# Layer 1 of a two-layer graph network on one core: the lower halves of x are taken against a copy in PSUM

## The chip, the core and the metric

The kernel runs on one core of a Trainium2 chip. The metric is device time in microseconds (us) for one execution. Before the change the median of 14 runs is 1414.99 us (1411.05 to 1419.32). TensorE (PE) multiplies and writes to PSUM, which has 8 banks of 512 f32 values in each of 128 partitions; VectorE (DVE) and ScalarE (ACT) read and write SBUF and PSUM; GpSimd (POOL) issues the gathers; SyncE (SP), ACT and POOL each issue DMAs in their own order. Each engine works through one list in order and meets the others at semaphores.

## What is computed

x has 6250 rows of 256 numbers. An edge list of 100,000 pairs (src, dst), sorted by dst, adds row src to row dst. The low dst numbers have by far the most edges.

```python
def _gin_agg(h, src, dst, eps, n_nodes):
    agg = jax.ops.segment_sum(h[src], dst, num_segments=n_nodes)
    return (1.0 + eps) * h + agg
...
h = _gin_agg(x, src, dst, eps1, n)         # layer 1, width 256
h = jax.nn.relu(h @ W1a + b1a)             # 256 -> 512
h = jax.nn.relu(h @ W1b + b1b)             # 512 -> 512
h = _gin_agg(h, src, dst, eps2, n)         # layer 2, width 512
h = jax.nn.relu(h @ W2a + b2a)
out = h @ W2b + b2b                        # 512 -> 256
...
x = _layernorm(x + out, axis=-1)
```

## The kernel before

Nodes are cut into 49 tiles of 128 (the last has 106), edges into 782 chunks of 128. After a preparation (index transposes, checks on the data) the program runs `layer` twice, for layer 1 and layer 2. The instruction order of every engine is fixed when the program is built, by a planner in Python: a clock that advances one `tick` per gathered chunk, work that is put off by some ticks (`later`), and two queues (`blockwise`, `beside`) that get credit with each chunk and spend it on work priced in estimated microseconds.

Three streams run beside each other in a layer.

- Gathers, for the edges of the lighter tiles: L270 issues one indirect DMA on POOL's queue per chunk, which brings the 128 rows named by `srcs` into one of `PIECES * BURST` = 24 places in the tile `early` (layer 1). The PE adds them up with a selection matrix (L1109). A gather into a place that is still used waits for the matmul that reads it, 24 chunks earlier. The sums leave PSUM through ACT (`split`, L1133), go through a second matmul (L1158) and are added to `acc` on DVE (L1147).
- Products, for the seven heaviest tiles (`HEAVY`): how often each source node occurs is counted in `counting` (DVE comparisons L939 and L942, matmul L985, DVE addition L955 into `at`). ACT turns the counts of one heavy tile and one range of four node tiles into the matrix `cf` (L970), and the PE multiplies it with the rows of x of that range (L885). To keep precision, x is handed to the PE in two halves of type f32r: an upper one (x rounded) and a lower one (x minus the upper), which stand side by side in the tile `both`. The heavy tiles are done in four passes, [6,5], [4], [3,2], [1,0], each over 13 ranges, so the halves are made 4 x 13 = 52 times, in `cut`. `both` has two buffers; `cut` is called for the current turn and the one after it before the current turn's matmuls are issued.
- Blocks of two finished tiles: transpose (L745), ACT copy to `zt` (L754), matmul with W1a (L777), ACT relu to `ht` (L786), matmul with W1b (L798), DVE bias (L1184), ACT relu (L1188), store of `h1`.

PSUM is handed out by the bank. `place` takes the first bank from the list `empty`; when the list is empty it first runs, at once, the put-off work that is due soonest among that which frees a bank. `take_later` puts off the reading of a bank by `LAG` = 10 ticks (7 for the sums of gathers), and `free` puts the bank at the end of the list.

```python
def place(n):
    while not empty:
        undelay(min((d for d in delayed if d[2]), key=lambda d: d[0]))
    i = empty.pop(0)
    return banks[i][:, :n], i
```

`halve` (L535, L536) makes the two halves: an ACT copy into the upper half, then a DVE subtraction. Layer 1 calls it from `cut` once per range for all four tiles (128 x 1024); layer 2 calls it from its own branch of `cut` and from `add_groups`, whose subtraction reads a PSUM bank (`split<-bank,split`).

Of the kernel before, what the change touches and what calls it, by code (L numbers as in the profile page):

```python
# [9 lines left out]
F32 = mybir.dt.float32  # L10
# [3 lines left out]
ALU = mybir.AluOpType  # L14
# [23 lines left out]
BANK = 512  # L38
# [108 lines left out]
def tile_gin_residual_layernorm(  # L147
# [38 lines left out]
    nc = tc.nc  # L186
# [104 lines left out]
    with tc.tile_pool(name="prep", bufs=2) as prep, tc.tile_pool(  # L291
# [76 lines left out]
        for i, c in enumerate(range(NC2, NCP, 512)):  # L368
            n = min(512, NCP - c)
# [6 lines left out]
        for g0, g1 in runs:  # L376
            c, h = groups[g0]
            n = g1 - g0
            a, b = c - NC2, c - NC2 + PARTS * h * n
            of_run = heads[:, a:b].rearrange("p (g b h) -> p g b h", b=PARTS, h=h)  # L380
            nc.vector.tensor_copy(base[:, g0:g1], of_run[:, :, 0, 0])
            for j in range(PARTS):
# [19 lines left out]
                op=ALU.subtract,  # L402
# [50 lines left out]
        for a, b, n in taken:  # L453
# [6 lines left out]
                op=ALU.subtract,  # L460
# [67 lines left out]
    def rows(t):  # L528
        return min(P, N - t * P)

    def halve(upper, lower, of):

        nc.scalar.copy(upper, of)  # L535
        nc.vector.tensor_tensor(lower, of, upper, op=ALU.subtract)  # L536
# [18 lines left out]
    def ordered(ctx):  # L555
# [9 lines left out]
        def layer(number, ctx, table, width, scale, wa, ba, wb, wide, prepare, finish, conclude, fetch):  # L565
# [110 lines left out]
            def undelay(item):  # L676
                delayed.remove(item)
                item[1]()
# [17 lines left out]
# [7 lines that stand above are left out]
            def free(p):  # L703
                empty.append(p[1])

            def take_later(p, what, lag=LAG):

                def take():
                    what(p[0])
                    free(p)  # L710

                later(lag, take, frees=True)
# [95 lines left out]
            def products(turns, table_of, ready=lambda t: True):  # L808

                loaded = {}  # L810
                factors = []
                sums = {}

                def load(i):
                    r, t = turns[i]
                    ks = ranges[r]
                    n = len(ks)
                    if (i == 0 or turns[i - 1][0] != r):
                        xr = dense.tile([P, RANGE, width], F32 if once else F32R, tag="xr", name="xr", bufs=2 if once else 2)
                        raw = xr if once else xr.bitcast(F32)  # L820
                        whole = min(n, N // P - ks[0])
                        if whole:
                            nc.sync.dma_start(
                                raw[:, :whole, :],
                                table[ks[0] * P : (ks[0] + whole) * P, :].rearrange(
                                    "(k p) d -> p k d", p=P
                                ),
                            )
                        if whole < n:
                            k = ks[-1]  # L830
                            nc.sync.dma_start(raw[: rows(k), whole, :], table[k * P : N, :])
                        loaded[0] = [xr, None, ks]
                    factors.append((loaded[0], None, table_of(r, ks, t)))

                def cut(of):


                    xr, upper, ks = of
                    if upper is not None:
                        return  # L840
                    if once:
                        of[1] = both = dense.tile([P, RANGE, 2, width], F32R, tag="both", name="both", bufs=2)
                        n = sum(rows(k) == P for k in ks)
                        for m, js in ((P, slice(0, n)), (rows(ks[-1]), slice(n, len(ks)))):
                            if js.start < js.stop:
                                halve(both[:m, js, 0, :], both[:m, js, 1, :], xr[:m, js, :])
                        return
                    of[1] = upper = dense.tile([P, RANGE, width], F32R, tag="upper", name="upper")
                    whole = xr.bitcast(F32)
                    for j, k in enumerate(ks):  # L850
                        m = rows(k)
                        halve(upper[:m, j, :], xr[:m, j, :], whole[:m, j, :])

                load(0)
                yield 0.0
                for i, (r, t) in enumerate(turns):
                    while len(factors) < 5 and i + len(factors) < len(turns):
                        new = turns[i + len(factors)][0] != turns[i + len(factors) - 1][0]
                        if once and new and sum(
                            f[0][1] is None and f[0] is not factors[k - 1][0]  # L860
                            for k, f in enumerate(factors)
                        ) >= 2:
                            break
                        load(i + len(factors))
                    while not ready(t):
                        yield 0.0
                    for f in range(min(2, len(factors))):
                        cut(factors[f][0])
                        if factors[f][2] and ready(turns[i + f][1]):
                            cf = dense.tile([P, RANGE, P], F32R, tag="cf", name="cf", bufs=3 if once else 4)  # L870
                            factors[f][2](cf)
                            factors[f] = factors[f][0], cf, None
                    (xr, upper, _), cf, _ = factors.pop(0)
                    ks = ranges[r]
                    opens = not once or r == 0
                    closes = not once or r == len(ranges) - 1
                    if opens:
                        sums[t] = place(2 * width if once else width)
                    pm = sums[t]
                    for j, k in enumerate(ks):  # L880
                        m = rows(k)
                        sides = (upper,) if once else (upper, xr)
                        for l, of in enumerate(sides):
                            of = of[:m, j]
                            nc.tensor.matmul(  # L885
                                pm[0], cf[:m, j, :],
                                of.rearrange("p a b -> p (a b)") if once else of,
                                start=(opens and j == 0 and l == 0),
                                stop=(closes and j == len(ks) - 1 and l == len(sides) - 1),
                            )  # L890

                    def add_product(ap, t=t):
                        for l in range(2 if once else 1):
                            nc.vector.tensor_tensor(
                                acc[t], ap[:, l * width : (l + 1) * width], acc[t], op=ALU.add
                            )
                        left[t] -= 1

                    if closes:
                        take_later(pm, add_product)  # L900
                    yield (4 if once else 2) * PASS * len(ks) * width
# [8 lines left out]
            def counting():  # L910
# [69 lines left out]
                def step():  # L980
# [12 lines left out]

                last = {t: END[ts[-1]] for ts in PASSES for t in ts}
                product = products(
                    [(r, t) for ts in PASSES for r in range(len(ranges)) for t in ts],
                    convert, lambda t: added > last[t],
# [75 lines left out]
            if number == 1:  # L1073
                work += 8.0 + STEP * NC + ADD * len(STEPS)
                aside = counting()
            else:
                aside = products([(r, t) for r in range(len(ranges)) for t in heavy],
                                     load_counts)
# [11 lines left out]
            both = (blockwise, beside)  # L1090
            upto = 0
            together_ = []
            for k, g in enumerate(order):
# [76 lines left out]
                if k + 2 < len(order):  # L1170
                    n = len(members[order[k + 1]])
# [339 lines left out]
```

## Time and profile before

One profiled execution took 1410.88 us, and its span (first to last instruction of the program) is 1409.2 us; the mean granted TensorE clock is 0.942 of full speed. All times of the trace are us from the start of the span.

| engine | busy us | share of the span | instructions |
|---|---|---|---|
| PE | 1204.7 | 85% | 5929 |
| DVE | 901.2 | 64% | 2267 |
| ACT | 486.8 | 35% | 892 |
| POOL | 1016.5 | 72% | 1034 |

| what | from | to |
|---|---|---|
| gathers of layer 1 (502) | 9.6 | 673.4 |
| upper halves on ACT, first and last start (L535) | 124.9 | 629.6 |
| subtractions on DVE, first and last start (L536) | 133.5 | 630.1 |
| gathers of layer 2 (518) | 705.2 | 1368.2 |

Between 673.4 and 705.2 POOL waits 31.8 us for the store of `h1`, whose rows layer 2 gathers. In the views a line of a group gives source line, engine, operation, out<-in by tile names, the count, then busy us and mean ns of one, then the idle time of the engine just before these instructions and what ended it. PE busy time is modelled and overlaps between matmuls, so a PE at 95% need not be at its peak. "Idle ... <-issue" means that nothing the profile shows was waited for.

### The profile page before, as it was taken

How to read it: one execution, taken by the hardware profiler on the slowest of the kernel's cores; microseconds unless marked ns; L12 is line 12 of the kernel's file. 1: busy time of each engine (PE TensorE's matmuls, PEld its weight loads, DVE VectorE, ACT ScalarE, POOL GpSimd, SP SyncE). 2: the span in 40 equal slices, each digit the busy share in tenths (PEclk: the TensorE clock that was granted, in tenths of full speed). 3: DMA queues.
4: the chain of work that ended last, by engine and by line, in shares of the span. 5: the costliest groups of instructions: out<-in, count | busy, mean ns of one | idle time of the engine just before them, and what ended most of it. 6: DMA issues, size and time to landing. Idle time of an engine off the chain costs nothing. (4 is left out here: it accounts for less than half of the span.)

```text
span 1409.2 us, 18558 instructions
## 1 busy us (share of the span) xinstructions
PE 1204.7 (85%) x5929; PEld 723.9 (51%) x5929; DVE 901.2 (64%) x2267; ACT 486.8 (35%) x892; POOL 1016.5 (72%) x1034
## 2 busy tenths in 40 slices
PE   2589999889898788788844999999989999997977
PEld 1144554444454443454521666676656666663646
DVE  7998778799968667332126577868856555553323
ACT  0223652444245332672314234333323333321112
POOL 6777777777777777777076777777777777777760
PEclk9989999899999999899977899999999999998989
DMA  4645766666457555674398699888889989877761
GB/s 102 199 135 182 240 205 178 188 205 203 146 182 223 169 153 153 218 224 131 114 352 286 204 302 302 267 295 286 254 286 303 302 273 341 256 229 239 223 203 40
DMA packets 159242, 309.77 MB, mean 220 GB/s; under 512 B 25378, under 2 KB 89762, under 8 KB 159136
## 3 DMA queue, kind: packets, MB, share of 16 engines
q0 software_dynamic: 65536, 201.65, 46.1%
q1 hardware_dynamic: 73060, 82.55, 18.3%
q10 hardware_dynamic: 20540, 24.28, 5.1%
q8 instruction: 50, 0.82, 0.2%
q14 instruction: 56, 0.46, 0.1%
HBM read 279.57 MB, written 28.83 MB: 219 GB/s over the span
## 5 line engine op out<-in xcount | busy, mean ns | idle before, releaser
L270 POOL DMA_INDIRECT early<-in_x_dram,srcs x502 | 511.1, 1018 | 159.0 <-issue 130.1
L270 POOL DMA_INDIRECT early<-h,srcs x262 | 254.8, 973 | 111.3 <-issue 62.7
L270 POOL DMA_INDIRECT late<-h,srcs x256 | 248.0, 969 | 80.7 <-issue 64.0
L1147 DVE SCALAR_TENSOR_TENSOR acc<-bank,mask,acc 128x512 f32<-128x512 f32 (+1 forms) x421 | 231.6, 606 | 89.6 <-PE bank L1158 89.3
L1109 PE MATMUL bank<-early,sel 128*32 128x256 f32 (+1 forms) x1528 | 161.4, 499 | 79.9 <-DMA early<-in_x_dram,srcs 31.5
L798 PE MATMUL bank<-w1b_s,ht 128*128 128x512 f32 (+1 forms) x392 | 181.1, 608 | 3.6 <-ACT ht L786 2.9
L777 PE MATMUL bank<-zt,w2a_s 128*128 128x256 f32 (+2 forms) x800 | 182.6, 385 | 1.1 <-ACT zt L754 1.1
L777 PEld LDWEIGHTS bank<-zt,w2a_s 128*128 128x128 f32 x800 | 152.7, 196 | 38.8 <-issue 10.0
L1158 PE MATMUL bank<-split,to 128*128 128x512 f32 (+3 forms) x362 | 122.4, 445 | 26.6 <-ACT split L535 23.0
L885 PE MATMUL bank<-upper,cf 128*128 128x512 f32 (+1 forms) x294 | 123.9, 421 | 12.5 <-ACT cf L906 11.7
L955 DVE TENSOR_TENSOR at<-bank,at 128x490 f32 x173 | 115.1, 666 | 11.9 <-ACT cf L970 4.2
L885 PE MATMUL bank<-both,cf 128*128 128x512 f32 (+1 forms) x343 | 111.1, 452 | 13.1 <-ACT ht L786 8.6
L798 PEld LDWEIGHTS bank<-w1b_s,ht 128*128 128x128 f32 (+1 forms) x392 | 74.3, 195 | 91.9 <-issue 76.2
L786 ACT ACTIVATE ht<-bank,b2a_s 128x256 f32<-128x256 f32 (+2 forms) x100 | 41.4, 465 | 221.1 <-PE bank L777 216.7
L1109 PEld LDWEIGHTS bank<-early,sel 128*32 128x32 f32 x1528 | 33.6, 112 | 163.6 <-issue 107.4
L885 PE MATMUL bank<-xr,cf 128*128 128x512 f32 (+1 forms) x294 | 116.2, 395 | 0.0
L1158 PEld LDWEIGHTS bank<-split,to 128*128 128x128 f32 (+1 forms) x362 | 67.0, 202 | 82.9 <-ACT split L535 33.9
L536 DVE TENSOR_TENSOR both<-xr,both 128x1024 fp32r<-128x1024 f32 (+1 forms) x52 | 60.3, 1160 | 66.2 <-ACT both L535 66.0
L942 DVE TENSOR_SCALAR cb<-numbers,spot 128x490 f16<-128x490 f16 x280 | 102.2, 365 | 0.0
L985 PE MATMUL bank<-cb,ca 128*128 128x490 f16 x280 | 90.1, 390 | 12.4 <-DVE acc L1147 6.2
L654 DVE TENSOR_TENSOR sel<-iota,slot 128x256 f32<-128x256 f32 (+3 forms) x119 | 51.4, 432 | 76.7 <-PE bank L1109 75.9
L777 PE MATMUL bank<-zt,w1a_s 128*128 128x256 f32 (+2 forms) x416 | 95.8, 379 | 4.6 <-DVE at L955 2.7
(132 smaller groups left out, 1551.3 us busy)
## 6 DMA issues: line engine op xcount, KB each, us to landing
xr<-in_x_dram SPq DMA_DIRECT2D x48, 512.0 KB
h<-h1r ACTq DMA_DIRECT2D x48, 256.0 KB
xr<-h SPq DMA_DIRECT2D x12, 1024.0 KB
acc<-h SPq DMA_DIRECT2D x23, 512.0 KB
counts<-ci ACTq DMA_DIRECT2D x72, 128.0 KB
ci<-counts SPq DMA_DIRECT2D x72, 128.0 KB
early<-in_x_dram,srcs POOLq DMA_INDIRECT x502
r<-in_x_dram SPq DMA_DIRECT2D x23, 256.0 KB
```

Source lines behind the costliest of these rows:

```text
L270: nc.gpsimd.indirect_dma_start(out=rows_[:, j, :], out_offset=None, in_=table, in_offset=bass.IndirectOffsetOnAxis(ap=srcs[:, c : c + 1], ...
L536: nc.vector.tensor_tensor(lower, of, upper, op=ALU.subtract)
L654: nc.vector.tensor_tensor(sel[:, :n, :], iota[:, :SLOTS].unsqueeze(1).to_broadcast([P, n, SLOTS]), slot[:, c0 : c0 + n].unsqueeze(2).to_br ...
L777: nc.tensor.matmul(ph[0][:, (f - o) * TILES * P : (f - o) * TILES * P + nb], wa[:, k, f * P : (f + 1) * P], zt[:, k, :nb], start=(k == 0), ...
L798: nc.tensor.matmul(po[0][:m], ht[:, f, i * P : i * P + m], wb[:, f, :], start=(f == 0), stop=(f == KH - 1),)
L885: nc.tensor.matmul(pm[0], cf[:m, j, :], of.rearrange("p a b -> p (a b)") if once else of, start=(opens and j == 0 and l == 0), stop=(close ...
L942: made = nc.vector.tensor_scalar(b, numbers, spot[:, c : c + 1], None, op0=ALU.is_equal)
L955: nc.vector.tensor_tensor(to, ap.rearrange("p (k w) -> p k w", w=W), to, op=ALU.add)
L985: mm = nc.tensor.matmul(pc[0], a, b, start=(i == 0), stop=(i == n - 1))
L1109: mm = nc.tensor.matmul(pm[b * SLOTS : (b + 1) * SLOTS], sel[:, c - c0, :], rows_[:, j, :], start=(c == parts[b][0]), stop=(c == parts[b][ ...
L1147: nc.vector.scalar_tensor_tensor(acc[t], ap[:, i * width : (i + 1) * width], mask[:, t - lo[g], g : g + 1], acc[t], op0=ALU.mult, op1=ALU.add,
L1158: nc.tensor.matmul(pu[0][:, i * width : (i + 1) * width], to[:used], split[:used, l, :], start=(once or l == 0), stop=(once or l == 1),)
```

## The change

In layer 1's branch of `cut` the call of `halve` is replaced. ACT still writes the upper halves of all four tiles at once. Then, for two tiles at a time (512 values, one bank), a new helper `less` takes a bank from `place`, ACT copies the upper halves into it, DVE subtracts the bank's content from x into the lower halves, and the bank is freed. The numbers computed are the same. Layer 2 still uses `halve`.

```diff
+                def less(lower, of, upper):
+                    p = place(BANK)
+                    m, n = of.shape[0], of.shape[1] * of.shape[2]
+                    there = p[0][:m, :n].rearrange("p (k d) -> p k d", d=width)
+                    nc.scalar.copy(there, upper.bitcast(F32))
+                    nc.vector.tensor_tensor(lower, of, there, op=ALU.subtract)
+                    free(p)
+
                 def cut(of):
...
                             if js.start < js.stop:
-                                halve(both[:m, js, 0, :], both[:m, js, 1, :], xr[:m, js, :])
+                                nc.scalar.copy(both[:m, js, 0, :], xr[:m, js, :])
+                                for a in range(js.start, js.stop, BANK // width):
+                                    b = min(a + BANK // width, js.stop)
+                                    less(both[:m, a:b, 1, :], xr[:m, a:b, :], both[:m, a:b, 0, :])
```

## The prediction

> **What bounds the kernel now.** I first asked the waits view what POOL waits for while layer 1 gathers (60 to 650 us), then for POOL's groups in the stretch that holds all 52 subtractions (130 to 640).
>
> ```profile
> POOL early L270 <- issue: 115.8, 380, 0.3
> POOL early L270 <- DMA early<-in_x_dram,srcs: 6.7, 22, 0.3
> ...
> L270 POOL DMA_INDIRECT early<-in_x_dram,srcs x384 | 394.9, 1028 | 117.0 <-issue 100.5 <-DMA early<-in_x_dram,srcs 5.5 <-PE bank L985 4.6
> ```
>
> The last number of a wait row is its longest: none is over 0.3 us. So POOL never waits for a place in `early`; it issues one gather after another, 0.95 us and a pause of 0.30, 1.25 us per chunk. 394.9 + 117.0 us fill the whole 510. The gathers are the metronome; time is lost where one takes longer than 0.95. The mean is 1.028, and this is where the difference comes from (timeline, POOL and DVE, first in layer 1, then in layer 2):
>
> ```profile
> 296.13 0.95 POOL L270 DMA_INDIRECT early<-in_x_dram,srcs  x1 [0.30 <-issue]
> 297.27 1.22 DVE L536 TENSOR_TENSOR both<-xr,both 128x1024 fp32r<-128x1024 f32 x1
> 297.38 1.93 POOL L270 DMA_INDIRECT early<-in_x_dram,srcs  x1 [0.30 <-issue]
> 299.62 0.95 POOL L270 DMA_INDIRECT early<-in_x_dram,srcs  x1 [0.30 <-issue]
> ```
>
> ```profile
> 1294.26 0.95 POOL L270 DMA_INDIRECT early<-h,srcs  x1 [0.30 <-issue]
> 1294.79 0.68 DVE L536 TENSOR_TENSOR split<-bank,split 128x512 fp32r<-128x512 f32 x1
> 1295.51 0.95 POOL L270 DMA_INDIRECT early<-h,srcs  x1 [0.30 <-issue]
> ```
>
> A gather that begins inside the subtraction `both<-xr,both`, whose two inputs lie in SBUF, ends 0.82 us after it (297.27 + 1.22 + 0.82 = 299.31 = 297.38 + 1.93). That is so in nearly every cut. I counted over the trace: 48 gathers begin inside one of these subtractions, and they last 20.3 us more than 48 x 0.947. The subtraction with one input in a PSUM bank does nothing of the kind: 47 gathers begin inside one, with a median of 0.947 us.
>
> Next, whether the consumers can follow a faster POOL: engine busy time by stage (columns: length, PE, PEld, DVE, ACT, POOL, then clock and DMA), and the only stage waits of the PE for gathers.
>
> ```profile
> 130.00:230.00 100.00, 95.40 (x466) 55.62 (x464) 74.67 (x181) 55.05 (x94) 76.84 (x77) 1.00 0.71 217
> 230.00:330.00 100.00, 86.02 (x400) 45.26 (x393) 89.58 (x229) 42.79 (x70) 77.40 (x75) 0.91 0.62 192
> 330.00:430.00 100.00, 91.20 (x443) 49.43 (x443) 83.83 (x243) 39.93 (x70) 77.20 (x75) 0.97 0.57 173
> 430.00:530.00 100.00, 80.95 (x381) 43.64 (x382) 65.92 (x201) 37.19 (x62) 76.97 (x76) 0.91 0.59 180
> 530.00:640.00 110.00, 92.62 (x455) 51.26 (x453) 53.26 (x134) 58.44 (x100) 84.90 (x83) 0.92 0.64 197
> ...
> PE bank L1109 <- DMA early<-in_x_dram,srcs: 15.1, 6, 5.7
> ...
> PE bank L1109 <- DMA early<-in_x_dram,srcs: 8.0, 4, 2.8
> ...
> PE bank L1109 <- DMA early<-in_x_dram,srcs: 6.4, 3, 3.3
> ```
>
> The three wait rows are of 430 to 530, 530 to 640 and 640 to 705; before 430 there is none. So to 430 the PE is nearly full and works off what POOL has put in the 24 places; afterwards it has room and waits for gathers, 29.5 us in all. The distance from a gather's end to its matmul says how full the places are: 2.3 us at the least, and about 25 before POOL would have to wait. It is 10 to 17 us near 120, 21.2 at its peak between 240 and 260, 3 to 12 near 430, 21.8 at its peak between 600 and 620, and 2 to 11 at 640 to 660.
>
> **The change, part by part.**
>
> *Removed:* 52 subtractions of two SBUF inputs (48 of 128x1024, 4 of 106x256). With them go the 20.3 us that POOL is held: 14 before 430, 6 after.
>
> *Added on ACT:* 100 copies from SBUF into a bank. No row shows that direction. Halving the 1024-wide copy (1048 ns) gives 524, the 512-wide copy SBUF to SBUF (`upper<-xr`) 623, PSUM to SBUF (`split<-bank`) 585 to 589; I take 0.60, as all 512-wide rows lie near it. 96 x 0.60 + 4 x 0.40 = 59 us; ACT goes from 233 to 292 of 510 us.
>
> *On DVE:* 100 subtractions in place of 52. The nearest row is `split<-bank,split`, 678 ns for 512 (666 to 688 among DVE's 512-wide additions with a bank): twice 0.68 for 1.22, 0.14 us more per cut. More counts that the two halves can't overlap: built and compared engine by engine, the changed program takes the *same* bank for both copies in 39 of the 48 full cuts, since `empty` is empty then and the bank just freed is the only one. So the order is copy (0.60), subtraction (0.68), copy (0.60), subtraction (0.68), with 0.03 us at each handover (before, the subtraction starts 0.03 after the ACT copy where DVE is idle). Where DVE waited for ACT, in the 27 cuts of the next row (what DVE sat idle for before L536: us, times), the lower half is done 0.60 + 0.03 + 0.68 + 0.03 + 0.60 + 0.03 + 0.68 - 1.22 = 1.4 us later; where DVE came late, 0.8 us later.
>
> ```profile
>   ACT both L535: 66.0, 27
> ```
>
> DVE's list is thus held up by 27 x 1.4 + 21 x 0.8 = 55 us at most, and ACT's by 52 x 1.9 = about 93 us (from the end of the upper copy: 0.60 + 0.03 + 0.68 + 0.03 + 0.60).
>
> *The new wait.* ACT now stands at the second copy until DVE reaches the first subtraction; behind it on ACT stand `cf` (L970), which the PE's products need, `split`, `zt` and `ht`. What hides this is that `cut` runs a turn ahead: matched cut by cut, the first product that reads a new `both` starts 7 us (median) after its subtraction; only 6 of 52 have under 1 us (one at 169, five at 582 to 630), which together cost the PE about 6 us. And DVE's 55 us lie in 143 us of idle DVE time between 130 and 640. The cover is thin from 230 to 430: DVE is busy 173 of 200 us, gets 18 cuts (8 x 1.4 + 9 x 0.8 = 18 us), and the same chunks are to be done in 191.
>
> *The banks.* `place` inside `cut` forces put-off reads to the front: on the PE some 200 of its layer 1 rows change places, and DVE and ACT meet some matmuls earlier than LAG wanted. No row prices that. At best banks come free sooner, and the 4 us that the PE waits for banks at L985 between 230 and 430 go; at worst DVE's waits for L798 in front of L1184, 31 us between 130 and 530 (7.9 + 4.7 + 9.8 + 9.0), double. I take 0, since most reads only move by a few places, and keep both ends for the range.
>
> *Moved DMAs:* no queue gets another DMA; POOL's gathers keep their order. Layer 2 is untouched, and starts when `h1` is stored, 31.8 us after the last gather.
>
> *A page against the row.* The Trainium skill (SBUF — State Buffer, Who interferes with whom) says that a VectorE instruction with two SBUF inputs contends only with GpSimd work that reads SBUF, and infers that `tensor_tensor` doesn't disturb descriptor generation, which needs the write side. By that the removal would bring nothing and the change could only cost; the 48 prolonged gathers say otherwise here, and I go by them.
>
> *The sum.* POOL gains 20.3 us if it never has to wait. The peaks decide: at 240 to 260 the distance was 21.2, POOL has gained 5 by then, so 26 against 25, 1 us lost, plus what the consumers lost before; at 600 to 620 it was 21.8, with 3 us gained since 555 and some 5 of the 6 us of short cuts, 30 against 25, 5 us lost. Taking a tenth of DVE's 55 us as reaching the PE where the cover is thin, another 1 to 2 us are lost near 250. Total 7 us given back, 13 left. What the PE is behind at 430 it can work off in the 29.5 us that it idles later, so the end of layer 1 follows POOL again. 1410.9 - 13 = 1397.9 for the profiled execution. That execution lies 4.1 us below the median, so 1402 for a median.
>
> **The rivals.**
>
> *All of it arrives* (0.13): no peak reaches the 24 places, 1415 - 20.3 = 1394.7. For it: slack of 7 us per cut. Against it: both peaks at 21 and more.
>
> *Swallowed* (0.14): the consumers are full until 430 and simply don't go faster. If half of DVE's 34 us before 430 (17 cuts x 1.4 + 12 x 0.8, about 34) reach the PE, POOL must wait 17 + 14 gained - 20 of room = 11 us, and another 5 to 9 at 610, which leaves 0 to 4: 1411 to 1415. For it: PE 91% and DVE 83% busy to 430.
>
> *ACT and DVE play ping-pong on one bank, and it lands on the PE* (0.23): all 34 us before 430 reach it. POOL waits 34 + 14 - 20 = 28 us there, which turns 14 gained into 14 lost; of the 6 gained later and the 23 us that DVE loses later within the 29.5 of idle PE, 6 to 8 come back: 1415 + 7 = 1422, and more where forced reads of banks add to it (half of their 31: 1437). It decides from the point where three quarters of DVE's added time show as PE time. For it: ACT and DVE have one list each, and ACT already waits 7 to 20 us per 100 for DVE in front of `cf`. Against it: the lead of the cuts.
>
> *A bank doesn't free POOL* would be the last, part of the slower case's chance: the 20.3 us stay and the ACT and DVE time comes on top, about 1425. The 47 undisturbed gathers speak against it.
>
> **How the numbers follow.** The main case, 5 to 19 us faster, gets 0.50: 1396 to 1410, likeliest 1402. Two thousandths, 2.8 us, is about what a measurement of this kernel can tell from no change. Faster: 0.50 + 0.13 and a little of the swallowed case, 0.64. Same 0.13. Slower 0.23. The range goes from 1393 (all arrives) to 1421, which takes in the swallowed case the good end of the banks and half of the slower one; some 0.15 is left outside.
>
> **What would show it.** In the new profile: mean of L270 in layer 1 down from 1018 to about 0.98 us, and no gather held beyond 0.95 by the halves' subtraction (step "removed"). Copies into the bank of 0.55 to 0.65 us, subtractions of 0.68, in the order copy, subtraction, copy, subtraction ("same bank"). POOL waits of some us for PE L1109 matmuls near 250 and 610, 7 us in all; over 20 us would mean the ping-pong case, none the full gain. The last gather of layer 1 at about 660 instead of 673.4, and still some 32 us from there to layer 2's first. Wrong altogether if gathers are still stretched in the cuts, or if the end of layer 1 comes later though POOL never waits.

## The result and the profile after

| kernel | median us | runs | lowest to highest |
|---|---|---|---|
| before | 1414.88 | 47 | 1410.67 to 1419.32 |
| changed | 1426.22 | 10 | 1424.31 to 1429.72 |

The ratio is 1.0082 (95% interval 1.007 to 1.0094): the change makes the kernel 11 us slower. The forecast was 1402 us and faster. The time is nearest to that of the rival in which ACT and DVE take turns on one bank and the PE feels it (1422).

The profiled execution has a span of 1425.1 us. Layer 2 takes 703.9 us from its first gather to the end before and 705.3 after, and the pause between the layers 31.8 and 32.0, so nearly all of the difference lies in layer 1: its last gather ends at 687.8 instead of 673.4 us, 14.4 us later. Where POOL's time goes there is in two views: first POOL's group in the page (busy us and mean ns, then the idle time before it), then POOL's waits from 60 to 720 us (us in all, times, longest).

```profile
L270 POOL DMA_INDIRECT early<-in_x_dram,srcs x502 | 487.8, 972 | 196.7 <-issue 132.8
```

```profile
POOL early L270 <- issue: 123.7, 406, 0.3
POOL early L270 <- DMA h<-h1r: 32.0, 1, 32.0
POOL early L270 <- PE bank L1120: 31.7, 16, 5.5
POOL early L270 <- PE bank L996: 16.4, 17, 6.4
```

The 502 gathers took 511.1 us before and take 487.8 now. The promised relief has come in full, 23.3 us: 52 gathers begin inside one of the new subtractions, and none of them is longer for it. But the second view has two rows which the kernel before had not. POOL, which never waited for a place in `early`, now waits 33 times for a matmul to give one back. Less the pause of 0.3 us that stands before every gather, that is 38.1 us. 38.1 - 23.3 = 14.8, against the 14.4 us by which layer 1 ends later. So the question is why the matmuls come late.

Matched by number, the matmul of gather 100 starts 4 us later than before, that of gather 200 19 us, of 300 32, of 400 19 and of 500 15. The loss arises between gathers 100 and 300 (296.5 us instead of 268.5) and about half of it is made good later. The windows show the same stretch (columns as before: length, PE, PEld, DVE, ACT, POOL, clock, DMA).

```profile
130.00:230.00 100.00, 88.53 (x419) 52.51 (x417) 64.47 (x158) 65.94 (x113) 75.10 (x80) 0.97 0.68 210
230.00:330.00 100.00, 79.24 (x332) 40.05 (x331) 79.42 (x207) 42.36 (x70) 62.65 (x66) 0.83 0.52 161
330.00:430.00 100.00, 86.83 (x391) 43.93 (x390) 83.51 (x239) 42.14 (x75) 67.48 (x71) 0.91 0.55 168
```

From 230 to 330 the PE does 332 matmuls where it did 400, DVE is *less* busy than before (79 against 90), and the clock is 0.83 instead of 0.91. No engine is full: they stand for each other. How, the timeline of one cut shows (start, us, engine, line; in brackets the idle time before it and what ended it; rows of POOL, of weight loads and of DMA issues are left out).

```profile
133.15 0.59 ACT L839 COPY bank<-both 128x512 f32<-128x512 f32 x1 [7.83 <-DVE h1t L1195]
...
139.32 1.04 ACT L854 CAST both<-xr 128x1024 fp32r<-128x1024 f32 x1 [0.40 <-ACT h1r L1199]
140.40 0.59 ACT L839 COPY bank<-both 128x512 f32<-128x512 f32 x1
141.02 0.69 DVE L840 TENSOR_TENSOR both<-xr,bank 128x512 fp32r<-128x512 f32 x1 [2.37 <-ACT bank L839]
141.74 0.59 ACT L839 COPY bank<-both 128x512 f32<-128x512 f32 x1 [0.75 <-DVE both L840]
142.26 1.13 ACT L981 CAST cf<-at 128x512 fp32r<-128x512 uint16 x2
142.36 0.69 DVE L840 TENSOR_TENSOR both<-xr,bank 128x512 fp32r<-128x512 f32 x1 [0.66 <-ACT bank L839]
...
143.10 3.78 PE L896 MATMUL bank<-both,cf 128*128 128x512 f32 x8 [5.01 <-DVE both L840]
```

From 140.40 on copy, subtraction, copy, subtraction follow each other, and each idle time of ACT and DVE in brackets names the other engine. `cf`, which the PE also needs, comes on ACT behind the second copy. The PE has stood for 5 us when the last subtraction ends. The first line, of an earlier cut, is the second kind of stand: ACT has waited 7.83 us because the bank for its copy still had to be read by DVE (`h1t`).

Over the whole of layer 1, for the copies on L839 (durations min/median/max, then what ACT stood for before them: us, times):

```profile
L839 ACT COPY bank<-both x100: 376/589/591, 133.1 to 653.8; 128x512 f32<-128x512 f32 x96, 106x256 f32<-106x256 f32 x4
...
  DVE both L840: 37.5, 38
  DVE at L966: 26.7, 10
  DVE h1t L1195: 14.4, 3
  DVE acc L1158: 6.7, 4
```

ACT stands 37.5 us for the subtraction, 38 times (the prediction counted 39 full cuts of 48 that use one bank twice), and 47.8 us for DVE to read what an earlier stage left in the bank (the last three rows). On the other side, from the same view of the subtraction on L840, first what DVE stood for, then who stood for the subtraction:

```profile
  ACT bank L839: 113.9, 85
...
  ACT bank L839: 37.5, 38
...
  PE bank L798: 7.8, 6
  PE bank L896: 7.8, 2
  PE bank L996: 5.1, 3
...
  PE bank L1120: 2.9, 1
...
  PE bank L1169: 1.7, 2
```

DVE stood 66.0 us for ACT here before and stands 113.9 now. Of the PE's rows only L896 reads the halves. The other four (17.5 us) don't; what they can want of the subtraction is the bank that it gives back. In the kernels f2 and f2b below, which borrow no bank, no matmul waits for the subtraction. So the borrowed bank has itself become something that the PE waits for.

A wait of the PE also shows in its clock. The same cut in four windows:

```profile
130.00:138.00 8.00, 7.94 (x40) 3.66 (x38) 6.23 (x15) 3.50 (x6) 6.06 (x7) 1.00 0.37 106
138.00:140.40 2.40, 0.09 (x1) 0.00 (x0) 0.65 (x2) 1.68 (x3) 1.89 (x2) 1.00 1.03 370
140.40:147.30 6.90, 4.20 (x16) 2.68 (x16) 4.97 (x13) 5.44 (x10) 5.08 (x6) 0.51 0.83 261
147.30:155.00 7.70, 7.70 (x46) 5.50 (x38) 4.84 (x12) 5.16 (x10) 5.87 (x7) 1.00 0.73 234
```

The PE stands still from 138.1, the clock falls to half at 140.4 and stays there for 6.9 us, 4.2 us beyond the end of the stall. Between 120 and 430 us such stretches sum to 23.9 us before and 58.0 after. 34 us more at half speed are up to 17 us of work not done; the waits of the PE that the profile names grow by 17 as well (27.8 to 45.1, those for DVE from 13.5 to 39.7). The two together are a little more than the 28 us lost; part of the slow stretches falls into the stalls themselves, as here, and so counts in both.

### The profile page after: what moved, and what is told of

Same layout as the page of the kernel before. It is cut to its first block, busy times and chain, and to the rows that moved or that the text cites. A ratio compares the mean times of both kernels' runs of the same rounds, so it can differ in the third digit from the quotient of the medians.

```text
span 1425.1 us, 18757 instructions
## 1 busy us (share of the span) xinstructions
PE 1213.9 (85%) x5929; PEld 725.7 (51%) x5929; DVE 907.6 (64%) x2315; ACT 543.6 (38%) x992; POOL 994.1 (70%) x1034
## 4 chain that ended last, share of the span: by engine, by line
PE 30%; DMA 10%; POOL 7%; issue 4%; DVE 1%; ACT 0%; POOLq 0%; SPq 0%; ACTq 0%
PE bank L777 9%; PE bank L896 6%; PE bank L798 6%; PE bank L1120 5%; DMA late<-h,srcs 5%; DMA early<-h,srcs 5%; POOL early L270 4%; POOL late L270 3%; PE bank L1169 2%; PE bank L745 1%; DVE acc L1158 0%; DMA early<-in_x_dram,srcs 0%; DVE xr L536 0%; ACT upper L535 0%; DMA h<-h1r 0%
## 5 line engine op out<-in xcount | busy, mean ns | idle before, releaser
L270 POOL DMA_INDIRECT early<-in_x_dram,srcs x502 | 487.8, 972 | 196.7 <-issue 132.8
L1120 PE MATMUL bank<-early,sel 128*32 128x256 f32 (+1 forms) x1528 | 159.3, 494 | 51.7 <-DMA early<-h,srcs 20.3
L840 DVE TENSOR_TENSOR both<-xr,bank 128x512 fp32r<-128x512 f32 (+1 forms) x100 | 66.8, 675 | 117.2 <-ACT bank L839 113.9
L896 PE MATMUL bank<-upper,cf 128*128 128x512 f32 (+1 forms) x294 | 124.0, 422 | 12.4 <-ACT cf L917 11.7
L896 PE MATMUL bank<-both,cf 128*128 128x512 f32 (+1 forms) x343 | 116.0, 465 | 21.4 <-ACT cf L981 10.6
L896 PE MATMUL bank<-xr,cf 128*128 128x512 f32 (+1 forms) x294 | 116.4, 396 | 0.0
L1120 PEld LDWEIGHTS bank<-early,sel 128*32 128x32 f32 x1528 | 33.1, 111 | 138.1 <-issue 78.1
L654 DVE TENSOR_TENSOR sel<-iota,slot 128x256 f32<-128x256 f32 (+3 forms) x119 | 51.4, 432 | 76.1 <-PE bank L1120 75.3
```

What stands on the lines that cost most here:

```text
L270: nc.gpsimd.indirect_dma_start(out=rows_[:, j, :], out_offset=None, in_=table, in_offset=bass.IndirectOffsetOnAxis(ap=srcs[:, c : c + 1], ...
L654: nc.vector.tensor_tensor(sel[:, :n, :], iota[:, :SLOTS].unsqueeze(1).to_broadcast([P, n, SLOTS]), slot[:, c0 : c0 + n].unsqueeze(2).to_br ...
L840: nc.vector.tensor_tensor(lower, of, there, op=ALU.subtract)
L896: nc.tensor.matmul(pm[0], cf[:m, j, :], of.rearrange("p a b -> p (a b)") if once else of, start=(opens and j == 0 and l == 0), stop=(close ...
L1120: mm = nc.tensor.matmul(pm[b * SLOTS : (b + 1) * SLOTS], sel[:, c - c0, :], rows_[:, j, :], start=(c == parts[b][0]), stop=(c == parts[b][ ...
```

## The experiments

The diffs are cut to the lines that matter, and are against the changed kernel unless said otherwise. "Held" is what gathers that begin inside a subtraction last beyond 0.947 us each, "POOL waits" what POOL waits for matmuls beyond its pause, both summed over one profiled execution. "Before" is the kernel before on the same chip.

| kernel | us | before | ratio (95%) | last gather of layer 1 | held | POOL waits |
|---|---|---|---|---|---|---|
| before | 1414.88 | | | 673.4 | 20.3 | 0 |
| changed | 1426.22 | 1414.88 | 1.0082 (1.007 to 1.0094) | 687.8 | 0 | 38.1 |
| f1 order only | 1403.43 | 1414.84 | 0.9921 (0.9892 to 0.995) | 665.7 | 15.1 | 0 |
| f2 copies, no bank | 1408.70 | 1414.84 | 0.9954 (0.9938 to 0.997) | 669.3 | 12.1 | 0.7 |
| f2b the same, taking turns | 1435.13 | 1414.84 | 1.015 (1.0114 to 1.0186) | 694.7 | 6.1 | 34.5 |
| f3 no subtraction | 1392.36 | 1414.84 | 0.9846 (0.9815 to 0.9878) | 652.7 | 0 | 0 |
| e4 two banks | 1404.32 | 1411.26 | 0.9948 (0.9929 to 0.9967) | 669.3 | 0 | 15.7 |
| j5 banks first | 1403.22 | 1413.21 | 0.9921 (0.9891 to 0.9951) | 668.9 | 0 | 17.6 |
| j1 split in two | 1404.57 | 1413.21 | 0.9944 (0.9924 to 0.9965) | 666.9 | 13.0 | 0 |
| k2 split in four | 1403.02 | 1411.25 | 0.9943 (0.992 to 0.9967) | 667.7 | 13.0 | 0 |
| k1 one bank, no turns | 1396.80 | 1411.25 | 0.9895 (0.9872 to 0.9919) | 659.9 | 4.0 | 0 |

Some kernels ran twice, because the first time they met chips on which the kernel before itself takes 1617 to 1634 us; these runs have a part of their own below.

### Is it the turns, the banks, the order, or DVE's work?

Four kernels take the change apart. The first leaves the banks and the order that they force on every engine, and takes the copies out:

```diff
                     p = place(BANK)
-                    ...
-                    nc.scalar.copy(there, upper.bitcast(F32))
-                    nc.vector.tensor_tensor(lower, of, there, op=ALU.subtract)
+                    nc.vector.tensor_tensor(lower, of, upper, op=ALU.subtract)
                     free(p)
```

> The program order of the changed kernel without its copies: the banks are taken and given back, but nothing is written to them, and DVE subtracts twice 512 values with both inputs in SBUF. Three theories of the loss. (Order) the reads that taking a bank forces to the front cost the time: then this kernel is slower than before too, 1425 us or more, as the relief of POOL is missing as well. (Bank wait) ACT stands at the copy until the bank's last reader on DVE is done: nothing stands here, so about as before, 1412 to 1419. (Added work) the copies and the second subtraction cost the time: no copies here, 1412 to 1419.

> The program order of the changed kernel without its copies (banks taken and given back, nothing written to them, two subtractions of 512 values with both inputs in SBUF), beside runs of before at 1411 to 1415 us. If the order that taking banks forces is the cause: 1424 us or more. If the alternation of copy and subtraction on one bank is, as e4_two_banks suggests: 1410 to 1420, since there is no copy to wait for, and POOL is held by the subtractions as before.

The second keeps the copies and takes no bank, so that the order of the PE is that of the kernel before. ACT copies to where the lower half will stand, and DVE subtracts in place:

```diff
-                    p = place(BANK)
-                    ...
+                    nc.scalar.copy(lower, upper.bitcast(F32))
+                    nc.vector.tensor_tensor(lower, of, lower, op=ALU.subtract)
```

> The program order of before with the two ACT copies and the two subtractions of 512, but without a bank: the copy goes to where the lower half will stand, and DVE subtracts in place. (Added work) 1425 us or more, since ACT and DVE have as much to do as in the changed kernel and POOL is still held. (Bank wait) and (Order): 1413 to 1421, a little over before for the 0.06 to 0.8 us that a cut takes longer on DVE.

> The program order of before with the two copies and two subtractions, no bank, and no alternation: copies go to where the lower half will stand. If the added work on ACT and DVE is the cause: 1424 or more. If the alternation is: 1410 to 1420.

The third is the second with one wait more per cut: the second copy may start only when the first subtraction has ended, as it must in the changed kernel where both use one bank. The instructions of every engine and their order are the same in these two. The diff is against the second:

```diff
-                def less(lower, of, upper):
-                    ...
+                def less(lower, of, upper, before=None):
+                    copy = nc.scalar.copy(lower, upper.bitcast(F32))
+                    if before:
+                        together(copy, [before])
+                    return nc.vector.tensor_tensor(lower, of, lower, op=ALU.subtract)
...
+                                done = None
...
-                                    less(both[:m, a:b, 1, :], ...)
+                                    done = less(both[:m, a:b, 1, :], ..., done)
```

> As e2_copies_no_bank, but the second copy waits for the first subtraction, as it does in the changed kernel where both use one bank. If this alternation is a large part of the loss, 5 us or more over e2_copies_no_bank; if the loss lies in the wait for the bank's earlier reader or in the order, within 3 us of it.

> As f2_copies_no_bank, but the second copy waits for the first subtraction, in the order of before and without a bank. If the alternation alone is the cause: 10 us or more over f2_copies_no_bank. If it costs only where the banks' order and the waits for earlier readers have used up the lead of the cuts: within 5 us of f2_copies_no_bank.

The fourth leaves the subtraction out; the lower halves are a second rounded copy of x on ACT. It no longer computes the layer and serves only to price the relief.

```diff
-                                for a in range(js.start, js.stop, BANK // width):
-                                    ...
+                                nc.scalar.copy(both[:m, js, 1, :], xr[:m, js, :])
```

> The subtraction is left out: ACT fills the lower halves by a second copy of x of 1024 values, the order is that of before and no bank is taken. It tells what POOL's relief is worth when nothing else is paid on DVE. If POOL is the metronome: 20 us less than before, 1393 to 1399, with gathers of 0.97 us in layer 1. If the PE can't follow a faster POOL anyway: 1404 or more, with POOL waiting for matmuls.

> The subtraction is left out (ACT fills the lower halves by a second copy of x), order of before, no bank. It tells what POOL's relief is worth when DVE pays nothing. Full relief: 20 us less than before, 1391 to 1396. If a part is given back because the PE fills the 24 places, 1398 to 1406, with POOL waiting for matmuls.

On the chip where the kernel before takes 1414.84, order alone gives 1403.43 and copies without a bank 1408.70: neither is slower. Without a subtraction it is 1392.36, so freeing POOL (and DVE) altogether is worth 22.5 us, near the 20.3 of the forecast's first term. And the one wait per cut turns 1408.70 into 1435.13: 26.4 us, with no instruction added, removed or moved. These rows are of what ACT waits for in layer 1 in f2b; the kernel without the wait has no such row:

```profile
ACT both L836 <- DVE both L839: 68.5, 45, 7.4
```

And this is what becomes of it on POOL, in f2 and then in f2b:

```profile
POOL early L270 <- issue: 120.4, 395, 0.3
POOL early L270 <- DMA early<-in_x_dram,srcs: 6.4, 21, 0.3
POOL early L270 <- PE bank L992: 5.8, 19, 0.3
POOL early L270 <- PE bank L1116: 4.0, 11, 0.9
```

```profile
POOL early L270 <- issue: 123.3, 404, 0.5
POOL early L270 <- PE bank L1121: 39.7, 19, 8.0
```

In f2 next to nothing is over the pause of 0.3; in f2b POOL waits up to 8 us for a place, as in the changed kernel. The windows from 230 to 330 of f2 and of f2b have the same mark too, with DVE less busy when it is slower:

```profile
230.00:330.00 100.00, 83.62 (x378) 43.13 (x379) 88.66 (x235) 48.49 (x81) 77.44 (x75) 0.93 0.62 184
```

```profile
230.00:330.00 100.00, 79.40 (x365) 42.61 (x364) 80.57 (x212) 46.30 (x78) 68.16 (x70) 0.90 0.54 166
```

The lead of the halves is the same in both (the first product that reads them starts 5.9 us after the subtraction in f2 and 5.8 in f2b, by the median), and between 120 and 430 us no matmul of f2b waits for a subtraction. What grows there from f2 to f2b are the PE's waits for other work of the two engines (for ACT, above all `ht` and `cf`, from 14.3 to 20.5 us, for DVE, above all `acc` and `at`, from 22.3 to 25.1) and its time at half clock (27.3 to 47.8 us).

So the turns alone, which f2b takes in all 48 full cuts, are enough for more than the whole loss. The changed kernel against f1 closes the account, as these two differ only in the copies, their waits and what the subtraction reads: gathers 503.4 to 487.8 (-15.6), waits of POOL 0 to 38.1, together +22.5; the last gather comes 22.1 us later, and the ratios (1.0082 and 0.9921) are 23 us apart.

### Undoing the turns and keeping the banks

If the turns are the cause, the relief should come through as soon as no engine has to come back to the same bank. Two banks are taken and both copies issued ahead of both subtractions (the new lines):

```diff
+                    parts = []
+                    for a in range(js.start, js.stop, BANK // width):
+                        p = place(BANK)
+                        ...
+                        nc.scalar.copy(there, both[:m, a:b, 0, :].bitcast(F32))
+                        parts.append((p, there, a, b))
+                    for p, there, a, b in parts:
+                        nc.vector.tensor_tensor(both[:m, a:b, 1, :], xr[:m, a:b, :], there, op=ALU.subtract)
+                        free(p)
```

> As the changed kernel, but two banks are taken before the two copies, both copies stand ahead of both subtractions, and each bank is given back after its subtraction, so the second copy does not wait for the first subtraction. If the alternation on one bank is the larger part of the loss: 1400 to 1412 where before takes 1415. If the loss lies in ACT standing at a copy until the bank's earlier reader on DVE is done, or in the order that taking banks forces, it stays or grows, since two banks are wanted at a time: 1424 to 1435.

It is faster than the kernel before, by 0.5%, and some 19 us faster than the changed one (ratios 0.9948 and 1.0082). Its copies stand for the bank's earlier readers as much as in the changed kernel; these are rows of ACT's waits in layer 1:

```profile
ACT bank L841 <- DVE at L970: 22.2, 11, 4.5
ACT bank L841 <- DVE h1t L1199: 22.0, 6, 8.0
...
ACT bank L841 <- DVE acc L1162: 8.5, 5, 3.8
```

52.7 us, against 47.8 in the changed kernel. So this stand is not what makes the difference; the row that is gone is the one for the subtraction. But the relief does not come through whole: POOL still waits 15.7 us for matmuls. Two reasons were weighed, the longer chain of a cut and the stand for the earlier readers. To shorten the chain the two copies were put first, straight from x, ahead of the upper halves (against the kernel with two banks):

```diff
+                        nc.scalar.copy(there.bitcast(F32R), xr[:m, a:b, :])
...
+                                less(both, m, js, xr)
                                 nc.scalar.copy(both[:m, js, 0, :], xr[:m, js, :])
```

> As e4_two_banks, but ACT rounds x straight into the two banks, before it writes the upper halves, so that DVE can begin 1.05 us earlier and the whole chain of a cut is about as long as before. If the length of the chain is what keeps e4_two_banks (1404) from the 1392 of f3_no_subtraction: 1393 to 1400. If ACT's wait for the banks' earlier readers is: 1401 to 1408, as e4_two_banks.

> As e4_two_banks, but ACT rounds x straight into the two banks, before it writes the upper halves, so that DVE can begin 1.05 us earlier. If the length of the chain is what keeps e4_two_banks (1404) from the 1392 of f3_no_subtraction: 1393 to 1400. If ACT's wait for the banks' earlier readers is: 1401 to 1408, as e4_two_banks.

That gave the same (1403.22 us, POOL waits 17.6), so beginning earlier brought nothing that can be told. The time is what was expected if the stand for the earlier readers is the reason: that stand is longer here (76.0 us on ACT, from the same three rows). But the kernel with one bank and no turns, below, has 51.4 us of it and POOL waits for no matmul. What keeps the rest with two banks stays open; the order that taking two banks at a time forces is another than f1's, and was not run by itself.

### How much is it worth to split the subtraction?

f1 was a puzzle: its subtractions read SBUF only, like those before, and it was 11 us faster. It differs from the kernel before in the order and in that the subtraction is cut in two. The kernel before with the cut alone, in two pieces and in four (`g2`, `k2`, one tile per piece):

```diff
-                                halve(both[:m, js, 0, :], both[:m, js, 1, :], xr[:m, js, :])
+                                nc.scalar.copy(both[:m, js, 0, :], xr[:m, js, :])
+                                for a in range(js.start, js.stop, 2):
+                                    at = slice(a, min(a + 2, js.stop))
+                                    nc.vector.tensor_tensor(
+                                        both[:m, at, 1, :], xr[:m, at, :], both[:m, at, 0, :], op=ALU.subtract)
```

> The kernel before with the subtraction cut into two of 512 values, both inputs in SBUF, nothing else changed. f1_order_only had this and the changed order and was 11 us faster than before. If the shorter holding of POOL explains that: 1403 to 1408 beside a before of 1411 to 1415, with some 15 us of prolonged gathers instead of 20. If the order that taking banks forces brings it: 1411 to 1417.

> The kernel before with the subtraction cut into two of 512 values, both inputs in SBUF, nothing else changed. f1_order_only had this and the changed order and was 11 us faster than before. If the shorter holding of POOL explains that: 1403 to 1408 beside a before of 1411 to 1415, with some 15 us of prolonged gathers instead of 20. If the order that taking banks forces brings it: 1411 to 1417.

> The kernel before with the subtraction cut into two of 512 values, both inputs in SBUF, nothing else changed. f1_order_only had this and the changed order and was 11 us faster than before. If the shorter holding of POOL explains that: 1403 to 1408 beside a before of 1411 to 1415, with some 15 us of prolonged gathers instead of 20. If the order that taking banks forces brings it: 1411 to 1417.

> As g1_split_in_two, in four subtractions of 256. If POOL gets in between two subtractions, the prolonged gathers cost 5 to 10 us and the time is 1398 to 1406; if a gather is held over several subtractions in a row, as in layer 2, it is no better than g1_split_in_two, 1403 to 1412.

> As j1_split_in_two, in four subtractions of 256. If POOL gets in between two subtractions, the prolonged gathers cost 5 to 10 us and the time is 1396 to 1403; if a gather is held over several subtractions in a row, no better than j1_split_in_two, 1402 to 1408.

Split in two it takes 1404.57 where the kernel before takes 1413.21: most of the gain of f1 is the split, and the forced order is worth the remaining 3 us or nothing, as the intervals overlap. POOL is held 13.0 us instead of 20.3. Four pieces hold it no less. POOL's groups of the two pages have the same busy time and mean:

```profile
L270 POOL DMA_INDIRECT early<-in_x_dram,srcs x502 | 504.9, 1006 | 158.8 <-issue 131.9
```

```profile
L270 POOL DMA_INDIRECT early<-in_x_dram,srcs x502 | 504.9, 1006 | 159.5 <-issue 131.1
```

The trace with four pieces shows why. Here are two cuts of it; the views merge the four pieces into one row (1.42 and 1.43 us):

```profile
176.48 1.42 DVE L849 TENSOR_TENSOR both<-xr,both 128x256 fp32r<-128x256 f32 x4
176.59 2.12 POOL L270 DMA_INDIRECT early<-in_x_dram,srcs  x1 [0.30 <-issue]
...
390.71 1.43 DVE L849 TENSOR_TENSOR both<-xr,both 128x256 fp32r<-128x256 f32 x4 [0.24 <-ACT both L846]
390.81 1.15 POOL L270 DMA_INDIRECT early<-in_x_dram,srcs  x1 [0.30 <-issue]
```

Both gathers begin 0.1 us into the first piece. The first ends 0.82 us after the fourth piece, so it was held over all four; the second ends 0.82 us after the first piece. Counted over layer 1, with two pieces 27 prolonged gathers end 0.82 us after the piece in which they began and are held 8.7 us in all, and 4 after the next piece, 3.4 us. With four pieces 21 end after their own piece, 3.4 us, and 9 after a later one, 7.5 us (one gather in each kernel fits neither). So the shorter pieces do shorten the hold where POOL gets in between, and lose it again where it does not, as the expectation's second case had it. What decides whether it gets in was not found.

### A version that beats both

From these findings a kernel follows in which neither engine waits for the other inside a cut: one bank, one copy. While ACT copies the upper halves of the first two tiles, DVE subtracts those of the other two from SBUF; then it takes the first two from the bank.

```diff
                     p = place(BANK)
...
+                    nc.scalar.copy(there, both[:m, a:c, 0, :].bitcast(F32))
+                    if c < js.stop:
+                        rest = slice(c, js.stop)
+                        nc.vector.tensor_tensor(
+                            both[:m, rest, 1, :], xr[:m, rest, :], both[:m, rest, 0, :], op=ALU.subtract)
+                    nc.vector.tensor_tensor(both[:m, a:c, 1, :], xr[:m, a:c, :], there, op=ALU.subtract)
                     free(p)
```

> One bank per cut and no alternation: ACT copies only the upper halves of the first two tiles into it, DVE meanwhile subtracts the other two tiles with both inputs in SBUF, then the first two from the bank. If one bank is harmless as long as no engine stands for the other in turns: 1396 to 1404, POOL held by about 7 us instead of 20. If taking a bank in a cut costs by itself, through ACT's wait for the bank's earlier reader: 1405 to 1412, with POOL waiting 10 us or more for matmuls.

1396.80 against 1411.25, 1.05% faster (0.81 to 1.28%). The timeline of a cut:

```profile
302.67 0.68 DVE L842 TENSOR_TENSOR both<-xr,both 128x512 fp32r<-128x512 f32 x1
302.84 0.59 ACT L839 COPY bank<-both 128x512 f32<-128x512 f32 x1 [7.58 <-DVE at L971]
302.87 1.30 POOL L270 DMA_INDIRECT early<-in_x_dram,srcs  x1 [0.30 <-issue]
...
303.46 0.69 DVE L845 TENSOR_TENSOR both<-xr,bank 128x512 fp32r<-128x512 f32 x1
...
304.47 0.95 POOL L270 DMA_INDIRECT early<-in_x_dram,srcs  x1 [0.30 <-issue]
```

ACT stood 7.58 us for the bank's earlier reader here as well, 51.4 us over the layer, and yet POOL waits for no matmul beyond its pause in this kernel. DVE works on the other half meanwhile, and starts on the bank 0.03 us after the copy. The gather that begins in the half from SBUF still takes 1.30 instead of 0.95; 4.0 us of holding are left over the layer. The PE's list is that of the changed kernel, instruction for instruction.

### The runs on other chips

On chips where the kernel before takes 1616.7, 1617.3 and 1634.3 us, the same kernels gave: order only 1.0024 (0.9992 to 1.0056), copies without a bank 1.0034 (1.0006 to 1.0062), taking turns 1.0108 (1.0067 to 1.0149), no subtraction 1.0025 (0.9995 to 1.0055), split in two 1.0013 (0.9984 to 1.0041) and 1.0007 (0.997 to 1.0045), split in four 1.001 (0.9979 to 1.004), banks first 1.0022 (0.9988 to 1.0057) and 1.0022 (0.998 to 1.0063). So what frees POOL brings nothing there, not even leaving the subtraction out, while the kernel with the turns is slower there too, by 13 us of the medians. In the trace of order only, POOL waits 66 us for matmuls in layer 1, and 34 us more for what the view calls only "remote": POOL is not what bounds the layer in this run. Its PE weight loads have stands of up to 9.8 us for which no record shows a reason (6.2 at the most in the profile of the kernel before). Why these chips are slower was not found, and the theories about POOL can't be judged from these runs.

## Why the prediction was wrong, step by step

- *POOL's gathers set the pace, and the subtraction of two SBUF inputs holds them*: right. The relief was put at 20.3 us and measured 23.3; the kernel without any subtraction was 22.5 us faster.
- *A subtraction with a bank doesn't hold them*: right, 52 gathers and none prolonged. The page of the Trainium skill that was weighed there (SBUF — State Buffer, Who interferes with whom) would have had no relief; the measurement decides against it.
- *Durations and order*: right. The copy was taken as 0.60 and took 0.589 us, the subtraction 0.68 and took 0.686, the handovers 0.03, and the turns on one bank were foreseen.
- *The forced order is worth nothing*: right within what can be told (f1 against j1).
- *The cover*: this is the step that failed. The forecast said "what hides this is that `cut` runs a turn ahead" and let "a tenth of DVE's 55 us" reach the PE. The lead of the products is really there and has hardly shrunk (median 7.4 us before, 6.0 after; under 1 us in 9 of 52 cuts instead of 6). It covers one of the things that come late, the products. It does not cover what is queued behind the copies and subtractions in the two lists: `cf`, `h1t`, the readers of banks, and the bank that the copy itself holds. f2 and f2b bear this out: the lead is the same in both (5.9 and 5.8 us), no matmul of f2b waits for the subtraction, and 26.4 us lie between them. DVE's extra stand for ACT came to 113.9 - 66.0 = 48 us, close to the bound of 55 (though f2, which is faster than the kernel before, has 86.3 - 66.0 = 20 us of it too). The PE's matmuls were 32 us late at gather 300, close to the 34 us that the rival let through, and POOL ended up waiting 38 us, where the forecast had 7 and named "over 20 us" as the sign of the rival.
- *What the prediction had no term for*: the granted clock. It took the PE's lateness as waits alone; with 34 us more at half clock the lateness was, by estimate, up to 17 us larger. And it took holding as all or nothing for the whole subtraction, so that the cheap edit, to split it, was not seen.
- *What is late at 430 can be worked off*: right in kind. The matmuls were 32 us late at gather 300 and 15 at gather 500. The rival used the same recovery. Its 28 us of waits for POOL up to 430 are nearly what was measured there (29.6); the 8.5 us after 430 it did not have, and its time (1422) was short by 4 us.
- *A slip in the working*: it takes 17 of the cuts before 430 as ones in which DVE waited for ACT. The waits view has 13 (7, 3 and 3 in the three stretches), which makes 31 us instead of 34. Nothing hangs on it.

## What to carry to other kernels

When a change makes two engines hand one buffer to and fro, price it by what stands behind the waiting instructions on both lists, not by the lead of its own result: the same instructions in the same order cost 26.4 us more with that one wait per cut. If a buffer has to be shared, give each engine something else to do in between, as k1 does, or give each copy its own place. And before a relief is bought with new work, try the cheap half of it: splitting one instruction in two gave 8.6 us with no other edit.

## What was not expected of the hardware

A subtraction of 128x1024 with two SBUF inputs held POOL's gathers 20.3 us in all; in two pieces of 512, 13.0 to 15.1 us; in four of 256, again 13.0, as a gather can be held over up to four pieces in a row.

The PE's clock fell to half without a full 3.4 us of idleness: at 140.4, when the PE had stood for 2.3 us; at 236.0, 1.9 us after a stall of 2.37 us and 0.7 us into one of 2.52; and at 270.1, 0.9 us after one of 2.74 us. In the 3.4 us before each of the seven falls between 120 and 430 us of the changed kernel the PE is idle for 1.5 to 2.5 us, as the trace models its busy time. The stretches last 3.4, 6.8, 10.2 or 13.7 us. The Trainium skill (TensorE: Matmul & The Clock Gate, What's actually happening) says that the clock is halved after an idle window of about 3.4 us, by a window that runs on its own. The lengths agree with it; the idleness that it names was not needed in these places.
